# From the scan loops to the first expert: the order of projections, turnings and router products, and where softmax and selection stand

## The chip, the cores and the metric

The kernel runs on one core of a Trainium2 chip. The metric is the device time of one execution in microseconds (us), lower is better. Before the change three timed runs took 1291.97 us in the median (1289.67 to 1293.01). A further execution was profiled; all places in time below are us from the start of its span.

## The reference, cut to what matters

The block takes 512 tokens (8 batches of 64, width 512) through three parts, each added to the residual x: cross attention, a pair of Mamba tracks (fast and slow), and a mixture of eight experts, of which each token takes two.

```python
# end of the second part: two tracks, mixed, projected, added
combined = w[0] * fast_out + w[1] * slow_out
x = x + combined @ proj_w.T + proj_b
# third part, on xt = layernorm(x)
logits = xt @ Wr + br
p = softmax(logits); probs, idx = top_k(p, 2); probs = probs / probs.sum(-1)
h = layernorm(relu(xt @ W1[e] + b1[e])) * g1[e] + be1[e]
y = layernorm(relu(h @ W2[e] + b2[e])) * g2[e] + be2[e]
x = x + sum over the two experts of probs * y
```

## The kernel before, in words

All matrices are float32. 512 tokens are four chunks (NT) of 128; a width of 512 is four blocks (ND) of 128. TensorE (PE) multiplies, VectorE (DVE) and ScalarE (ACT) work on the results, GpSimd (POOL) and SyncE (SP) issue most DMAs.

**End of the Mamba part (L1126 to L1189).** The scan loops run over two tracks, eight channel blocks and six groups of states. After them come four output products (`rest_of`, m = 0 to 3) of the last channel block, each into one bank of two PSUM tiles of three banks: m = 0 and 1 into `das[0]`, m = 2 and 3 into `das[1]`. After each, DVE adds it to `comb[m]` (L1146). `projected(c)` then multiplies `comb` with `proj_w` for chunk c (L1159; `pp` alternates between the two single-bank tiles `mm` and `yp`), adds it to the residual `xr` on DVE (L1162) and normalizes it (L1164 to L1171, with the square root on ACT) into `l3`, which has the memory of `oT`. `routed(c)` turns the chunk with four PE transposes into the third bank of `das[c % 2]` (L1176), copies them on ACT to `xT` (L1177), multiplies with the router's matrix `wr` into a strip of the first bank of `das[0]` (L1180) and adds the bias on DVE to `pr` (L1183).

**The choice of experts (L1257 to L1403).** From `pr` of all chunks DVE finds the two best experts of a token (`hots`), counts (`upto`, with the PE products `rank` and `count`), and makes `take`, with which PE gathers the first expert's rows (`gp`, L1297, copied by ACT into `xgT0`, L1300). The rows of the others are scattered by eight indirect DMAs of POOL into `x_rows` in HBM (L1352) and fetched again expert by expert (`xg`, L1433). The softmax over the experts (`ex`, from L1371, exponential on ACT) is needed for the gates and for `share`.

**The experts.** Expert p has an `up` half (`hp` = L1470, activation on ACT L1477), twice; its centring, scaling and `down` (L1520) stand beside the next expert's `up`. Its rows are turned by PE at L1439. `selection()` makes, for the last expert, four `give` tiles on DVE (L1409), turns them on PE (L1413) and copies them on ACT into `put` (L1414); it is called in the second expert's first half.

**What sets the order.** Instructions wrapped in `keep(...)` stay on their engine in the order of the program among one another; the others are placed by the framework's scheduler, which weighs estimated times and dependences. Dependences are kept by tile: an instruction that writes one bank of `das[0]` waits for the reader of another bank of it. Tiles take turns in a fixed number of buffers. Weight loads of the experts are issued by SP (L1225, L1233); they use memory that the loops hold until the last router product.

Of the kernel before, what the change touches and what calls it, by code (L numbers as in the profile page):

```python
# [13 lines left out]
ALU = mybir.AluOpType  # L14
# [6 lines left out]
NT = T // P  # L21
ND = D // P
# [27 lines left out]
def perceiver_block(ctx: ExitStack, tc: tile.TileContext, a: dict, out: bass.AP):  # L50
    nc = tc.nc

    keep = tc.keep_in_program_order
# [7 lines left out]
    ident = const.tile([P, P], F32, name="ident")  # L61
# [152 lines left out]
    pr = const.tile([P, NT, E], F32, name="pr")  # L214
# [8 lines left out]
    def block(general):  # L223
# [4 lines left out]
        with ExitStack() as ctx:  # L228
# [594 lines left out]
            with tc.tile_pool(name="mb1", bufs=1) as mb1, tc.tile_pool(name="mb2", bufs=2) as mb2, tc.tile_pool(  # L823
# [304 lines left out]
                def rest_of(m, chunks):  # L1128
                    for i in chunks:
                        keep(nc.tensor.matmul(  # L1130
                            das[m // 2][:, m % 2, :], mos[m][:, i, :], xs[1][i], start=(i == m + 4), stop=(i == last)
                        ))
# [8 lines left out]
                    summed_up(q)  # L1141
                for m in range(2, ND):
                    rest_of(m, range(m + 4, last))
                for m in range(ND):
                    rest_of(m, [last])
                    keep(nc.vector.scalar_tensor_tensor(  # L1146
                        comb[m], das[m // 2][:, m % 2, :], tw[:, 1:2], comb[m], ALU.mult, ALU.add
                    ))
# [7 lines left out]
                def projected(c):  # L1156
                    pp = pm.tile([P, D], F32, tag=("mm", "yp")[c % 2], name="pp")
                    for k in range(ND):
                        keep(nc.tensor.matmul(  # L1159
                            pp, comb[k][:, c * P : (c + 1) * P], pws[k], start=(k == 0), stop=(k == ND - 1)  # L1160
                        ))
                    keep(nc.vector.tensor_tensor(xr[:, c, :], xr[:, c, :], pp, ALU.add))  # L1162
                    st = small.tile([P, 6], F32, tag="lnst1", name="lnst1")
                    keep(nc.vector.bn_stats(st, xr[:, c, :]))  # L1164
                    mv = small.tile([P, 2], F32, tag="lnmv1", name="lnmv1")
                    keep(nc.vector.bn_aggr(mv, st))
                    std = small.tile([P, 1], F32, tag="std1", name="std")
                    keep(nc.scalar.activation(std, mv[:, 1:2], AF.Sqrt, bias=eps))
                    rs = small.tile([P, 1], F32, tag="rs1", name="rs")
                    keep(nc.vector.reciprocal(rs, std))  # L1170
                    keep(nc.vector.tensor_scalar(l3[:, c, :], xr[:, c, :], mv[:, 0:1], rs, ALU.subtract, ALU.mult))  # L1171

                def routed(c):
                    tp = das[c % 2][:, 2, :]
                    for k in range(ND):
                        keep(nc.tensor.transpose(tp[:, k * P : (k + 1) * P], l3[:, c, k * P : (k + 1) * P], ident))  # L1176
                    keep(nc.scalar.copy(xT[:, c, :], tp))  # L1177
                    rp = das[0][:, 0, c * E : (c + 1) * E]
                    for k in range(ND):
                        keep(nc.tensor.matmul(  # L1180
                            rp, xT[:, c, k * P : (k + 1) * P], wr[:, k, :], start=(k == 0), stop=(k == ND - 1)
                        ))
                    keep(nc.vector.tensor_tensor(pr[:, c, :], br, rp, ALU.add))  # L1183

                projected(0)
                for c in range(1, NT):
                    projected(c)
                    routed(c - 1)
                routed(NT - 1)  # L1189

            mbx.close()

# [5 lines left out]
            with ExitStack() as moe:  # L1198
# [43 lines left out]
                with tc.tile_pool(name="mor", bufs=1) as mor:  # L1242
                    def over_e(t):
                        return t.rearrange("p (c o) -> p c o", o=1).to_broadcast([P, NT, E])
# [4 lines left out]
                    def tiny(name):  # L1249
                        return mor.tile([P, NT], F32, name=name)  # L1250

                    def wide(name, n=NT):
                        return mor.tile([P, n, E], F32, name=name)
# [3 lines left out]
                    hots, tops = [], []  # L1257
                    for i in range(2):
                        src = left if i else pr
                        m = tiny(f"top{i}")  # L1260
# [33 lines left out]
                    for k in range(ND):  # L1294
                        gp = pe.tile([P, CAP], F32, tag=("tp", "yp")[k % 2], name="gp")
# [72 lines left out]


                    ex = wide("ex")  # L1370
                    nc.vector.tensor_tensor(ex, pr, over_e(tops[0]), ALU.subtract)  # L1371
                    nc.scalar.activation(ex, ex, AF.Exp)
                    ls = tiny("ls")
                    nc.vector.tensor_reduce(ls, ex, AX.X, ALU.add)
# [30 lines left out]
                def selection():  # L1405

                    for c in range(NT):
                        give = mo2.tile([P, P], F32, tag="y", name="give")
                        nc.vector.tensor_scalar(  # L1409
                            give, iota[:, :P], place7[:, c : c + 1], share[:, c : c + 1], ALU.is_equal, ALU.mult  # L1410
                        )
                        gp = pe.tile([P, P], F32, tag="tp", name="gp7")
                        nc.tensor.transpose(gp, give, ident)  # L1413
                        nc.scalar.copy(put[:, c * P : (c + 1) * P], gp)  # L1414

                for p in range(1, E):
# [182 lines left out]
                def experts(todo):  # L1599
# [3 lines left out]
                    for p, s0 in todo + [(E, 0)]:  # L1603
# [8 lines left out]
                        for hf in range(2):  # L1612
                            if p < E:
                                up(hf, st)
                            if (p, s0, hf) == (1, 0, 0) and first:
                                selection()
                            if prev is not None and not (p == E and first and hf == 0):
                                for i in range(2):
                                    (center, scale)[hf](i, prev[2])
# [27 lines left out]
            with tc.If(rare > 0):  # L1647
# [10 lines left out]
                if not general:  # L1658
                    with tc.If(flag(found[0:1, 1:2], 1) > 0):
                        block(True)  # L1660

    block(False)


# [54 lines left out]
```

## Time and profile before

| | |
|---|---|
| timed runs, median (range) | 1291.97 us (1289.67 to 1293.01) |
| the profiled execution, its own time | 1286.84 us |
| its span in the trace | 1285.1 us |
| mean granted TensorE clock | 0.977 of full speed |
| PE busy | 1183.2 us (92%) |
| DVE busy | 800.9 us (62%) |
| ACT busy | 592.9 us (46%) |
| POOL busy | 502.2 us (39%) |

The profiled execution's own time is 1.74 us over its span and 5.13 us under the median of the timed runs. A float32 product appears in the trace as two passes (x2), and a wait in brackets behind an instruction is the idle time of its engine before it, with what ended it. PEld is PE's loading of weights, SPq the queue of SyncE.

### The profile page before, as it was taken

How to read it: one execution, taken by the hardware profiler on the slowest of the kernel's cores; microseconds unless marked ns; L12 is line 12 of the kernel's file. 1: busy time of each engine (PE TensorE's matmuls, PEld its weight loads, DVE VectorE, ACT ScalarE, POOL GpSimd, SP SyncE). 2: the span in 40 equal slices, each digit the busy share in tenths (PEclk: the TensorE clock that was granted, in tenths of full speed). 3: DMA queues.
4: the chain of work that ended last, by engine and by line, in shares of the span. 5: the costliest groups of instructions: out<-in, count | busy, mean ns of one | idle time of the engine just before them, and what ended most of it. 6: DMA issues, size and time to landing. Idle time of an engine off the chain costs nothing. (4 is left out here: it accounts for less than half of the span.)

```text
span 1285.1 us, 14205 instructions
## 1 busy us (share of the span) xinstructions
PE 1183.2 (92%) x5134; PEld 720.4 (56%) x5134; DVE 800.9 (62%) x1135; ACT 592.9 (46%) x1265; POOL 502.2 (39%) x353
## 2 busy tenths in 40 slices
PE   5999999999987899999899998978799999999996
PEld 5444454444543333334333333333589999999994
DVE  5144444444666999999999999995415244333363
ACT  2233334333227576677666665651126235334460
POOL 5100000000015688888798888870130201221102
PEclk9999999999988999999999999999799999999998
DMA  6429910000007110101431010010395725746634
GB/s 213 164 63 300 302 36 1 1 1 1 1 9 263 63 32 2 33 1 57 180 116 33 16 50 17 25 41 17 127 399 200 285 107 211 300 176 229 259 127 129
DMA packets 94160, 147.36 MB, mean 115 GB/s; under 512 B 5888, under 2 KB 63504, under 8 KB 89984
## 3 DMA queue, kind: packets, MB, share of 16 engines
q1 hardware_dynamic: 88496, 130.26, 29.6%
q0 software_dynamic: 4528, 14.00, 3.0%
q10 hardware_dynamic: 1056, 2.10, 0.5%
q8 instruction: 42, 0.69, 0.2%
q14 instruction: 38, 0.31, 0.1%
HBM read 121.80 MB, written 24.54 MB: 114 GB/s over the span
## 5 line engine op out<-in xcount | busy, mean ns | idle before, releaser
L1114 POOL TENSOR_TENSOR db<-r,bc 128x1536 f32<-128x1536 f32 (+1 forms) x96 | 294.8, 3077 | 51.1 <-DVE da L1076 34.8
L1076 DVE TENSOR_TENSOR_SCAN da<-da,db 128x1536 f32<-128x1536 f32 (+1 forms) x96 | 288.1, 3001 | 7.6 <-POOL db L1114 5.8
L1090 PE MATMUL yp<-hc,ident 128*128 128x512 f32 x512 | 239.8, 604 | 16.3 <-DVE hc L1080 16.3
L1110 ACT ACTIVATE da<-dt,an 128x504 f32<-128x504 f32 x256 | 175.3, 685 | 10.0 <-DVE dt L892 0.8
L1090 PEld LDWEIGHTS yp<-hc,ident 128*128 128x128 f32 x512 | 95.6, 191 | 149.3 <-issue 106.3
L1080 DVE TENSOR_TENSOR hc<-da,bc 128x1536 f32<-128x1536 f32 (+1 forms) x96 | 151.7, 1580 | 10.3 <-PE yp L1090 1.6
L1470 PE MATMUL hp<-xgT,w 128*128 128x192 f32 (+3 forms) x1024 | 147.6, 303 | 5.8 <-DVE xgT L1442 3.0
L1470 PEld LDWEIGHTS hp<-xgT,w 128*128 128x128 f32 x1024 | 143.0, 191 | 7.6 <-DVE xgT L1442 3.7
L1520 PE MATMUL yp<-h,w 128*128 128x192 f32 (+3 forms) x1024 | 146.4, 303 | 0.9 <-DMA w<-in_w_dram 0.6
L1520 PEld LDWEIGHTS yp<-h,w 128*128 128x128 f32 x1024 | 143.2, 191 | 2.3 <-ACT h L1500 0.8
L450 POOL COPY qbd<-qT 32x256 f32<-32x256 f32 x32 | 12.6, 395 | 214.0 <-PE sp L631 207.3
L1610 POOL DMA_DIRECT2D ev<-in_ev_dram x8 | 4.5, 569 | 231.8 <-ACT yT L1527 178.1
L460 PE MATMUL kp<-ctx,wk 128*128 128x400 f32 x256 | 93.6, 510 | 0.0
L617 PE MATMUL vp<-wv,ctx 128*128 128x512 f32 x192 | 88.2, 604 | 0.0
L1477 ACT ACTIVATE h<-hp,ev 128x192 f32<-128x192 f32 (+3 forms) x128 | 50.1, 393 | 77.5 <-PE hp L1470 77.0
L680 DVE COPY oT<-op 32x64 f32<-32x64 f32 x64 | 13.7, 214 | 96.7 <-PE op L669 96.3
L930 PE MATMUL ip<-oT,iw 128*128 128x512 f32 x128 | 61.2, 623 | 12.1 <-issue 5.4
L1105 ACT COPY da<-zeros 128x24 f32<-128x24 f32 (+1 forms) x96 | 16.9, 176 | 117.9 <-DVE hc L1080 117.9
L460 PEld LDWEIGHTS kp<-ctx,wk 128*128 128x128 f32 x256 | 46.3, 189 | 43.7 <-issue 13.7
L1537 DVE BATCH_NORM_STATS2 bs<-ytp 128x6 f32<-128x512 f32 (+3 forms) x13 | 8.5, 689 | 90.0 <-PE ytp L1535 90.0
L637 DVE CUSTOM_DVE_ANT_0 sc<-sp,madd,rsc 128x400 f32<-128x400 f32 x64 | 38.1, 629 | 40.4 <-PE sp L631 40.4
L1038 PE MATMUL cp<-x,mo 128*128 128x512 f32 x108 | 50.2, 598 | 7.9 <-ACT r L874 7.9
(292 smaller groups left out, 1617.7 us busy)
## 6 DMA issues: line engine op xcount, KB each, us to landing
w<-in_w_dram SPq DMA_DIRECT2D x64, 1024.0 KB, 15.8
bc<-bcd SPq DMA_DIRECT2D x8, 1536.0 KB, 9.4
x_rows<-z SPq DMA_DIRECT2D x8, 1152.0 KB, 12.1
y_rows<-z SPq DMA_DIRECT2D x8, 1152.0 KB, 12.2
ctx<-in_ctx_dram SPq DMA_DIRECT2D x32, 200.0 KB, 4.3
iw<-in_fast_in_w_dram SPq DMA_DIRECT2D x8, 512.0 KB, 6.6
iw<-in_slow_in_w_dram SPq DMA_DIRECT2D x8, 512.0 KB, 3.4
mo<-in_slow_mout_w_dram SPq DMA_DIRECT2D x8, 512.0 KB, 3.7
```

The source lines that it names most:

```text
L460: nc.tensor.matmul(kp[:, :n], wk[:, k, ec * P : (ec + 1) * P], ctx_t[k][:, o : o + n], start=(k == 0), stop=(k == ND - 1),)
L617: nc.tensor.matmul(vp, ctxs[b][k][:, j * P : (j + 1) * P], wv[:, k, :], start=(k == 0), stop=(k == ND - 1))
L930: keep(nc.tensor.matmul(s[key], w[:, k, u * P : (u + 1) * P], oT[k], start=(k == 0), stop=(k == ND - 1)))
L1038: keep(nc.tensor.matmul(s["cp"], mo[:, i, :], xs[t2][i], start=(i == 0), stop=(i == n - 1)))
L1076: keep(nc.vector.tensor_tensor_scan(hs, hs, q["db"][:, :w, :].rearrange("p n s -> p (n s)"), 0.0, ALU.mult, ALU.add))
L1080: keep(nc.vector.tensor_tensor(q["hc"][:, :w, :], q["da"][:, :w, :], bcs[t][1][n][:, 1], ALU.mult))
L1090: keep(nc.tensor.matmul(yp[0], ident, q["hc"][:, j, :], start=False, stop=(n + j == NS - 1)))
L1110: keep(nc.scalar.activation(by_batch(da[:, j, :])[:, :, 1:], by_batch(dt)[:, :, 1:], AF.Exp, scale=an[:, t, k : k + 1]))
L1114: keep(nc.gpsimd.tensor_tensor(db[:, :w, :], du.rearrange("p (o s) -> p o s", o=1).to_broadcast([P, w, T]), bc[:, 0], ALU.mult))
L1470: nc.tensor.matmul(hp, st["w1"][k][:, i * P : (i + 1) * P], st["xgT"][:, k, :n], start=(k == 0), stop=(k == ND - 1),)
L1477: nc.scalar.activation(h[:, i, :], hp, AF.Relu, bias=st["ev"][:, i : i + 1])
L1520: nc.tensor.matmul(yp, ws[i // 4][:, i % 4, m * P : (m + 1) * P], st["h"][:, i, :], start=(i == 0), stop=(i == NF - 1),)
```

## The change

Four edits in the stretch between the scan loops and the second expert:

- the four output products and combinations run in the order 0, 2, 1, 3, so that the two PSUM tiles take turns;
- `routed` is split: `turned(c)` holds the transposes and the copy to `xT`, `routed(c)` the router's product. Two projections come first, and then for each chunk its turning, the projection two chunks on, and its router product;
- the first instruction of the softmax (`ex`, L1371) is kept in program order, behind the other kept DVE work;
- the transposes of `selection` (L1413) are kept in program order too.

In the built kernel this moves, beyond the loops: on DVE the softmax and what hangs on it, from between the sums of `upto` to behind the last flag (`either`, L1367); on ACT the table load and exponential from before the copies of `xgT0` to between the third and fourth of them; on PE the four transposes of `selection` from among the first expert's first products to among the second expert's, near its mean; with them the copies to `put` on ACT and two of the four `give` on DVE. The queues of SP and POOL keep their order and their waits.

```diff
--- before.py
+++ after.py
@@ -1141,7 +1141,7 @@
                     summed_up(q)
                 for m in range(2, ND):
                     rest_of(m, range(m + 4, last))
-                for m in range(ND):
+                for m in (0, 2, 1, 3):
                     rest_of(m, [last])
                     keep(nc.vector.scalar_tensor_tensor(
                         comb[m], das[m // 2][:, m % 2, :], tw[:, 1:2], comb[m], ALU.mult, ALU.add
@@ -1170,11 +1170,13 @@
                     keep(nc.vector.reciprocal(rs, std))
                     keep(nc.vector.tensor_scalar(l3[:, c, :], xr[:, c, :], mv[:, 0:1], rs, ALU.subtract, ALU.mult))
 
-                def routed(c):
+                def turned(c):
                     tp = das[c % 2][:, 2, :]
                     for k in range(ND):
                         keep(nc.tensor.transpose(tp[:, k * P : (k + 1) * P], l3[:, c, k * P : (k + 1) * P], ident))
                     keep(nc.scalar.copy(xT[:, c, :], tp))
+
+                def routed(c):
                     rp = das[0][:, 0, c * E : (c + 1) * E]
                     for k in range(ND):
                         keep(nc.tensor.matmul(
@@ -1182,11 +1184,14 @@
                         ))
                     keep(nc.vector.tensor_tensor(pr[:, c, :], br, rp, ALU.add))
 
+
                 projected(0)
-                for c in range(1, NT):
-                    projected(c)
-                    routed(c - 1)
-                routed(NT - 1)
+                projected(1)
+                for c in range(NT):
+                    turned(c)
+                    if c + 2 < NT:
+                        projected(c + 2)
+                    routed(c)
 
             mbx.close()
 
@@ -1368,7 +1373,7 @@
 
 
                     ex = wide("ex")
-                    nc.vector.tensor_tensor(ex, pr, over_e(tops[0]), ALU.subtract)
+                    keep(nc.vector.tensor_tensor(ex, pr, over_e(tops[0]), ALU.subtract))
                     nc.scalar.activation(ex, ex, AF.Exp)
                     ls = tiny("ls")
                     nc.vector.tensor_reduce(ls, ex, AX.X, ALU.add)
@@ -1410,7 +1415,7 @@
                             give, iota[:, :P], place7[:, c : c + 1], share[:, c : c + 1], ALU.is_equal, ALU.mult
                         )
                         gp = pe.tile([P, P], F32, tag="tp", name="gp7")
-                        nc.tensor.transpose(gp, give, ident)
+                        keep(nc.tensor.transpose(gp, give, ident))
                         nc.scalar.copy(put[:, c * P : (c + 1) * P], gp)
 
                 for p in range(1, E):
```

## The prediction

> **What bounds the kernel now.** I read the page first (PE is busy 92% of the span), then the chain of waits in order of time. From 939.85 us to the end that chain is PE's, nearly without a break; in the stretch that the change touches, 884 to 940 us, it hops between PE, DVE and ACT. So I read this stretch instruction by instruction. From the timeline (start, duration, engine, line, operation, tiles, then idle time before it and who ended it):
>
> ```profile
> 885.97 1.98 PE L1130 MATMUL da<-x,mo 128*128 128x512 f32 x4 [0.84 <-DVE comb L1146]
> 887.13 1.61 DVE L1146 SCALAR_TENSOR_TENSOR comb<-da,tw,comb 128x512 f32<-128x512 f32 x2 [1.22 <-PE da L1130]
> 888.80 1.12 PE L1130 MATMUL da<-x,mo 128*128 128x512 f32 x2 [0.84 <-DVE comb L1146]
> ...
> 896.62 0.60 PE L1176 MATMUL da<-ident,oT 128*128 128x128 f32 x4
> 898.70 0.57 ACT L1177 COPY xT<-da 128x512 f32<-128x512 f32 x1
> 899.31 1.06 PE L1180 MATMUL da<-wr,xT 128*128 128x8 f32 x8 [2.09 <-ACT xT L1177]
> 900.23 5.38 PE L1159 MATMUL pp<-pw,comb 128*128 128x512 f32 x8
> 908.19 1.06 PE L1180 MATMUL da<-wr,xT 128*128 128x8 f32 x8 [2.15 <-ACT xT L1177]
> 909.10 3.68 PE L1159 MATMUL pp<-pw,comb 128*128 128x512 f32 x8
> 915.37 1.06 PE L1180 MATMUL da<-wr,xT 128*128 128x8 f32 x8 [2.15 <-ACT xT L1177]
> 917.59 1.87 PE L1180 MATMUL da<-wr,xT 128*128 128x8 f32 x8 [0.68 <-ACT xT L1177]
> ```
>
> PE stands twice for a combination (L1146) before it may write the neighbouring bank of the same tile, and three times some 2.1 us for xT, since the router's product is queued right behind the turning that feeds it. Nothing else runs: DVE and ACT are on the same thread.
>
> Then the start of the first expert, and the gather of the second expert's rows with its landing (last line: the list of DMA issues; last number is us to landing):
>
> ```profile
> 934.66 0.38 PE L1413 MATMUL gp<-ident,give 128*128 128x128 f32 x2
> 937.63 0.27 ACT L1414 COPY put<-gp 128x128 f32<-128x128 f32 x1 [1.21 <-PE hp L1470]
> 939.00 0.27 ACT L1414 COPY put<-gp 128x128 f32<-128x128 f32 x1 [1.10 <-PE hp L1470]
> 939.37 0.73 ACT L1477 ACTIVATE h<-hp,ev 128x192 f32<-128x192 f32 x2
> 939.85 10.34 PE L1470 MATMUL hp<-xgT,w 128*128 128x192 f32 x62 [2.25 <-ACT h L1477]
> 951.23 1.12 POOL L1433 DMA_DIRECT2D xg<-x_rows  x2 [12.96 <-DMA w<-in_w_dram]
> 958.89 1.86 PE L1439 MATMUL xtp<-ident,xg 128*128 128x128 f32 x8
> ...
> xg<-x_rows POOLq DMA_DIRECT2D x3, 256.0 KB, 6.1
> ```
>
> The selection's transposes and copies stand among the first expert's products; its activation waits behind them on ACT, and the third product waits for that. And the second expert's rows are close behind PE: issued at 951.23 and 951.78, landed by 957.9 if these too take 6.1 us, used at 958.89.
>
> **The change, part by part** (us in the frame of this execution).
>
> 1. Combinations 0, 2, 1, 3. A product is two passes of 0.43. Products 0 and 2 now run from 884.00 without a wait (different tiles). Combination 0 ends at 885.91 as before; product 1 starts at 885.97. Product 2, from 884.86, is out 1.16 later as product 0 was (884.00 to 885.16), so combination 2 ends 886.77 and product 3 starts at 886.85 instead of 888.80. The first projection follows at 887.85 instead of 889.76: **-1.9**. If the second wait stayed: -0.8.
>
> 2. Loops. Before: projection 0, 1, turn 0, router 0, projection 2, and so on. After: p0 p1 t0 p2 r0 t1 p3 r1 t2 r2 t3 r3. Start of t0: 16 passes after p0, at 894.73 (l3 of chunk 0 is out at 894.24, the row's 896.14 less 1.9: no wait). t0 0.57, p2 3.44 (eight passes of 0.43), r0 at 898.74: xT of chunk 0 is out at 899.27 less 1.9 = 897.4, so no wait. r0 0.8, t1 0.57, p3 3.44 end at 903.55; xT of chunk 1 stands behind std of chunk 2 on ACT (about 900.9), done by 901.5: no wait. r1 ends 904.4. Here comes a new wait. t2 writes the tile that r1 has just written, and pr of chunk 1 must read it first; on DVE's queue that reading now stands behind the whole normalization of chunk 3, which takes 3.0 from the end of p3 (rows: 912.82 to 915.63, plus pr 0.16). So t2 starts about 906.7, PE idle 2.3; queued behind it are r2, t3 and r3, and for r3 waits the whole expert stage. Then t2 to r2 1.3, r2 0.85, t3 to r3 1.3 (row: 916.28 to 917.59): r3 at 910.15 instead of 917.59. Of these 7.4, 1.9 are part 1's: **-5.5**. In it are two waits of 2.1 that vanish, 1.9 that p2 loses at present (5.38 against 3.44, at half clock, below), and a longer end (r1's end to r3 5.75, where p3's end to r3 took 4.97). Bounds: -3.0 if p2 had been at full clock anyway and r2 falls into a half-clock stretch (0.85 more); -6.4 if r3 runs at full clock.
>
> What waits for r3: the first weight load of the experts on SP (919.59, idle until then on the router's product) and ev on POOL's queue. Neither queue changes its order. So loads, scatter and gather move with r3.
>
> 3. Softmax held back. Its subtraction, and with it 12 small DVE operations, leave the chain to "take". The fourth sum (L1279) goes from 923.45 to about 923.03, and the division of the gates (L1387) no longer stands between: gp some 0.2 earlier, **-0.2**, between 0 and -0.5. On ACT the exponential's table load (1.28) and the exponential (0.23) now stand between the third and fourth copy of xgT0. Hidden: the fourth is needed only by the fourth product step, some 2 us after gp's end; without that cover it costs at most 0.6.
>
> 4. Selection held back. From 933.2 to 939.85 PE passes 16 products at 0.163 and four transposes: 3.1 us of work in 6.6. Without transposes and copies the products take 2.6, so up to 3.3 is won at the first expert. But PE would come to L1439 at 958.89 less all this, and the rows move only with parts 1 to 3. Their slack is 1.0 (957.9 against 958.89): **-0.9**, the rest becomes a wait for the rows of about 2.4. Bounds 0 and -3.3.
>
> 5. Selection's new place: in the order of the built kernel PE's queue now holds two transposes after the second expert's mean product (975.67) and two after half of the next tile. The first two cost 0.22. The third waits for its "give" on DVE, which stands behind the sum of squares (976.67, 0.96) and runs to about 978.0: PE, there at 977.75, waits 0.3; the fourth 0.3 more; then the second variance product waits for a DVE sum moved back by two "give" (0.7). By adding: products that stood at 979.03 stand at 979.98: **+0.95**. Queued behind: the sigma, scale and down-projection follow 0.8 later, still ahead of PE. Bounds: 0.45 (the four transposes' work alone) and 3.3 (what they cost at the old place).
>
> Sum: -1.9 - 5.5 - 0.2 - 0.9 + 0.95 = **-7.55**. The profiled execution took 1286.84 (span 1285.1 and 1.74 outside it); it becomes 1279.3. The median 1291.97 lies 5.13 above that execution, and I keep the distance: 1284.4. After 960 us PE is busy 97 to 99% and the loads are released by its progress, so the gain is carried to the end.
>
> **Clock.** From the windows view (PE busy, ..., then granted clock, DMA share, GB/s):
>
> ```profile
> 897.00:900.40 3.40, 1.31 (x12) 1.09 (x10) 2.10 (x5) 0.77 (x2) 0.00 (x0) 1.00 0.00 0
> 900.40:903.80 3.40, 3.40 (x5) 1.39 (x5) 0.16 (x1) 0.00 (x0) 0.00 (x0) 0.52 0.00 0
> 914.10:917.50 3.40, 1.55 (x12) 1.31 (x12) 1.20 (x5) 1.31 (x3) 0.00 (x0) 1.00 0.00 0
> 917.50:920.90 3.40, 1.87 (x8) 1.78 (x8) 1.23 (x8) 0.65 (x2) 0.78 (x2) 0.51 0.30 39
> ```
>
> Here stretches with PE busy 1.31 and 1.55 of 3.4 were followed by half clock, and no wait in them was longer than 2.4. [...]
>
> **Rivals.** (a) The wait for the rows halves the clock: a wait of 2.4 can leave a stretch like those two; the next 3.4 at half clock costs 1.7: 1286.1. For: the rows above. Against: only if part 4 really wins its 3.3, and by the place of the stretch.
> (b) Rows come earlier than PE needs (the scatter is faster, or the wait at t2 is shorter): part 4 gives up to 3.3: about 1282.
> (c) Loops gain less (-3.0) and the selection costs 3.3 at its new place: -1.9 - 3.0 - 0.2 - 0.9 + 3.3 = -2.7: 1289.3. For: transposes in PE's queue with DVE and ACT between them are what cost 3.3 at present.
> (d) Slower: the rows do not move. From 935 to 960 the DMA engines are full (shares 1.00 to 1.06), and the gather stood 12.96 on POOL. If the scatter's landing is set by the bytes already queued and not by its issue, PE wins only 0.9, stands over 7 us at L1439, then runs at half clock (13.65 us of it, as from 917.5 to 931.2, costs up to 6.8), and pays 0.95: +0.05 to +6.8: 1292 to 1299, about 1296. It decides once the rows land less than 3 us earlier. Against: the bytes ahead of the scatter are released by r3 as well.
> (e) The loops give nothing: what is taken from xT comes back in full at the turnings behind pr. Then 5.5 of the 7.55 is gone: 1289.9.
>
> **Numbers.** Forecast 0.46, (a) 0.22, (b) 0.08, (c) 0.12, (d) 0.08, (e) 0.04. A measurement of this kernel can tell 0.3% (3.9 us) from no change, so faster is below 1288.1 and slower above 1295.9. Faster: forecast, (a), (b) and a little of (c): 0.78. Same: most of (c), (e), a third of (d): 0.17. Slower: 0.05. Range 1280.5 to 1290.5: down to (b) less the 1.5 of a clock kept full at r3, up to (c) and (e); (d) is left out.
>
> **What would show it.** PE's waits for xT at the first two router products gone; a wait of some 2.3 at the third turning, ended by DVE pr; SP's first weight load about 7.4 earlier, at 912.2; no "put" among the first expert's products and its first activation about 3 us sooner after gp; a wait at L1439 (L1444 then) for the rows, which land about 7.6 earlier; transposes of the selection near the second expert's mean with waits under 1 us in all. Wrong if the first weight load is less than 5 us earlier, if t2 starts without a wait, if the rows land less than 5 us earlier, or if PE loses over 2 us at the selection's new place.

## The result and the profile after

Five executions of each kernel: before 1290.2 us median (1289.3 to 1293.01), after 1283.92 us (1281.8 to 1287.98); after/before 0.9947, 95% interval [0.9923, 0.997]. Timed again, with the second pair of profiles below: 1287.29 before, 1279.44 after, 0.994 [0.9919, 0.996].

The first profile of the changed kernel is of the slowest of its five executions (1287.98 us), and it was already 1.9 us behind the profile of before at the scan's last products, where nothing is changed; so the two are compared by distances inside a stretch. First the timeline of PE in it (start, duration, engine, line, operation, tiles, idle time before it and who ended that):

```profile
884.92 4.97 PE L1130 MATMUL da<-x,mo 128*128 128x512 f32 x10
889.73 7.03 PE L1159 MATMUL pp<-pw,comb 128*128 128x512 f32 x16
...
900.47 0.95 PE L1182 MATMUL da<-wr,xT 128*128 128x8 f32 x8
...
905.18 0.95 PE L1182 MATMUL da<-wr,xT 128*128 128x8 f32 x8
908.32 0.65 PE L1176 MATMUL da<-ident,oT 128*128 128x128 f32 x4 [2.18 <-DVE pr L1185]
909.64 1.88 PE L1182 MATMUL da<-wr,xT 128*128 128x8 f32 x8 [0.68 <-ACT xT L1177]
911.37 1.09 PE L1176 MATMUL da<-ident,oT 128*128 128x128 f32 x4
913.14 1.88 PE L1182 MATMUL da<-wr,xT 128*128 128x8 f32 x8 [0.67 <-ACT xT L1177]
...
927.02 2.11 PE L1475 MATMUL hp<-xgT,w 128*128 128x192 f32 x12
930.59 0.89 PE L1475 MATMUL hp<-xgT,w 128*128 128x192 f32 x4 [1.46 <-DMA w<-in_w_dram]
935.00 1.33 PE L1475 MATMUL hp<-xgT,w 128*128 128x192 f32 x3 [3.52 <-ACT h L1482]
```

The combinations' two waits are gone (ten passes, which are five products, in one row), and so are the first two waits for xT. The third turning has the new wait, 2.18 for DVE pr. From 909.55 on the windows view gives a granted clock of 0.50: 1.88 for a router product that takes 0.95 in the row at 905.18. At the end stands something that the prediction has not: PE is through with the first 16 passes of the first expert at 931.5 by its own records, and the first activation is not until 934.52 (the last row is cut by the end of the window asked for). The timeline of ACT in the same profile shows it, and the same once more at the very end of the kernel:

```profile
934.52 0.73 ACT L1482 ACTIVATE h<-hp,ev 128x192 f32<-128x192 f32 x2 [6.53 <-remote]
...
1268.74 0.37 ACT L1532 ACTIVATE yT<-yp,ev 128x128 f32<-128x128 f32 x1 [7.66 <-remote]
```

"Remote" is a releaser that the profile can't name. PE's last records before these two end at 931.5 and 1264.6, 3.0 and 4.2 earlier. The first profile of before has the same at these two places, 1.8 at each. So both kernels were profiled once more; there neither profile has these delays. This second pair (1287.41 us before, 1278.82 after, spans 1285.75 and 1277.16) is the clean one. In it the first weight load of the experts (SPq), the first activation (ACT), and PE at the first and second expert, the kernel before:

```profile
920.39 10.42 SPq L1225 DMA_DIRECT2D w<-in_w_dram  x8
937.24 0.73 ACT L1477 ACTIVATE h<-hp,ev 128x192 f32<-128x192 f32 x2
...
934.13 1.46 PE L1470 MATMUL hp<-xgT,w 128*128 128x192 f32 x8
935.43 0.38 PE L1413 MATMUL gp<-ident,give 128*128 128x128 f32 x2
935.65 0.82 PE L1470 MATMUL hp<-xgT,w 128*128 128x192 f32 x4
936.31 0.51 PE L1413 MATMUL gp<-ident,give 128*128 128x128 f32 x2
936.66 0.82 PE L1470 MATMUL hp<-xgT,w 128*128 128x192 f32 x4
937.71 10.34 PE L1470 MATMUL hp<-xgT,w 128*128 128x192 f32 x62 [0.24 <-ACT h L1477]
...
958.25 0.33 PE L1439 MATMUL xtp<-ident,xg 128*128 128x128 f32 x1 [1.34 <-DMA xg<-x_rows]
959.18 2.41 PE L1439 MATMUL xtp<-ident,xg 64*128 64x64 f32 x7 [0.60 <-DMA xg<-x_rows]
961.52 4.21 PE L1470 MATMUL hp<-xgT,w 128*128 128x192 f32 x12
```

and the changed kernel:

```profile
914.56 10.24 SPq L1230 DMA_DIRECT2D w<-in_w_dram  x8
931.25 0.73 ACT L1482 ACTIVATE h<-hp,ev 128x192 f32<-128x192 f32 x2 [2.30 <-PE hp L1475]
...
927.99 2.96 PE L1475 MATMUL hp<-xgT,w 128*128 128x192 f32 x16
931.73 10.34 PE L1475 MATMUL hp<-xgT,w 128*128 128x192 f32 x62 [0.78 <-ACT h L1482]
...
951.99 0.34 PE L1444 MATMUL xtp<-ident,xg 128*128 128x128 f32 x1 [1.00 <-DMA xg<-x_rows]
952.95 1.66 PE L1444 MATMUL xtp<-ident,xg 64*128 64x64 f32 x7 [0.62 <-DMA xg<-x_rows]
954.53 2.22 PE L1475 MATMUL hp<-xgT,w 128*128 128x192 f32 x12
...
970.26 0.38 PE L1418 MATMUL gp<-ident,give 128*128 128x128 f32 x2
970.48 0.82 PE L1462 MATMUL var<-s,mean_f 128*128 128x192 f32 x4
971.13 0.81 PE L1475 MATMUL hp<-xgT,w 128*128 128x192 f32 x4
971.90 0.55 PE L1418 MATMUL gp<-ident,give 128*128 128x128 f32 x2
```

Read them against the prediction: at the old place the selection's four transposes stand among the first expert's products, and the first activation comes 16.85 after the first weight load; without them, in the changed kernel, 16.69. So they cost next to nothing (3.3 was predicted to hang on them). At their new place no row has a wait for give. PE waited for the second expert's rows in the kernel before too (1.34 and 0.60), and after it the products ran at half clock (4.21 against 2.22 for the same twelve passes). The windows view (PE busy first; granted clock, DMA share and GB/s last), the stretch with that wait and the next one, before and after:

```profile
955.88:959.30 3.42, 1.48 (x9) 1.00 (x7) 0.00 (x0) 0.62 (x2) 0.10 (x1) 1.00 1.07 349
959.30:962.71 3.41, 3.41 (x11) 2.29 (x12) 2.43 (x4) 0.00 (x0) 0.81 (x2) 0.50 1.02 340
```

```profile
949.65:953.07 3.42, 1.80 (x11) 1.32 (x9) 0.00 (x0) 0.84 (x2) 0.09 (x1) 1.00 1.05 342
953.07:956.48 3.41, 3.41 (x19) 2.78 (x20) 2.36 (x4) 0.00 (x0) 1.08 (x2) 1.00 1.04 351
```

The ledger of the second pair, each row a difference of two starts in PE's timeline (the last rows by ACT's):

| distance | before | after | change | predicted |
|---|---|---|---|---|
| first product of the slow scan's output projection (da, L1130) to first projection (pp) | 12.78 | 10.82 | -1.96 | -1.9 |
| first projection to last router product | 27.83 | 23.42 | -4.41 | -5.5 |
| last router product to first product of the first expert's gather (gp) | 7.41 | 7.17 | -0.24 | -0.2 |
| that to the second expert's first transpose (xtp) | 32.45 | 32.26 | -0.19 | -0.9 |
| that to the first expert's second mean product | 7.27 | 4.60 | -2.67 | 0 |
| that to the second expert's first mean product | 13.25 | 12.95 | -0.30 | 0 |
| that to the first expert's first yT (selection's new place in it) | 17.12 | 17.72 | +0.60 | +0.95 |
| first yT to end | 289.86 | 289.90 | +0.04 | 0 |
| upstream of all this | | | +0.55 | |
| sum | | | -8.58 | -7.55 |

### The profile page after: what moved, and what is told of

Read it like the earlier page. It is cut to its first block, busy times and chain, and to the rows that moved or that the text cites. A ratio compares the mean times of both kernels' runs of the same rounds, so it can differ in the third digit from the quotient of the medians.

```text
span 1286.2 us, 14209 instructions
## 1 busy us (share of the span) xinstructions
PE 1183.3 (92%) x5134; PEld 722.6 (56%) x5134; DVE 802.3 (62%) x1135; ACT 592.2 (46%) x1265; POOL 502.2 (39%) x353
## 5 line engine op out<-in xcount | busy, mean ns | idle before, releaser
L1475 PE MATMUL hp<-xgT,w 128*128 128x192 f32 (+3 forms) x1024 | 150.2, 306 | 8.5 <-ACT h L1482 4.0
L1475 PEld LDWEIGHTS hp<-xgT,w 128*128 128x128 f32 x1024 | 145.6, 193 | 10.6 <-ACT h L1482 4.6
```

Source lines behind the costliest of these rows:

```text
L1475: nc.tensor.matmul(hp, st["w1"][k][:, i * P : (i + 1) * P], st["xgT"][:, k, :n], start=(k == 0), stop=(k == ND - 1),)
```

## The experiments

Times are in us; each ratio is against the kernel before on the same chip (e1 to e6 and the second pair on one chip, e7 to e9 on a second, e10 on a third; one profile of each). "da to r3" is the distance in PE's timeline from the first product of the slow scan's output projection to the last router product, "load" the first weight load of the experts.

**e1, the orders alone; e2, the held-back operations alone.**

```diff
 e1 (changed kernel)                        e2 (kernel before)
-keep(nc.vector.tensor_tensor(ex, ...))    +keep(nc.vector.tensor_tensor(ex, ...))
+nc.vector.tensor_tensor(ex, ...)          -nc.vector.tensor_tensor(ex, ...)
-keep(nc.tensor.transpose(gp, give, ...))  +keep(nc.tensor.transpose(gp, give, ...))
+nc.tensor.transpose(gp, give, ...)        -nc.tensor.transpose(gp, give, ...)
```

> The kernel before with parts 1 and 2 alone (order of the combinations, and the order of the loops); softmax and selection are as before. Theory A (the prediction's steps): third turning waits about 2.2 for DVE pr, first weight load of the experts 6.4 earlier against the last scan product than before, selection's transposes still among the first expert's products, and the first activation 19.8 after the first weight load as before; after the first expert about 0.8 of the gain is kept more than in the changed kernel, because nothing is paid at the second expert: about -7.4 against before in all. Theory B (the first expert starts when its own four weight tiles are in, 15.4 after the first load, and the selection's place is not what sets it): the same distances, about -6.4 + 0.9 less the half clock: 1284 to 1285.5. The two part in e2, not here; what this run must show by both is a gain within 1.5 us of the changed kernel's, and if it is under 3 us the loops are not the source of the gain.

> The kernel before with softmax and selection held back alone (parts 3, 4, 5). Theory A: without transposes and copies among the first expert's products its first activation comes about 16.5 after the first weight load (19.8 before), and PE then waits about 2.3 at the second expert's transposes for its rows, whose landing does not move. Total -0.2, plus up to 1.7 if that wait halves the clock. Theory B: first activation still 19.4 after the first weight load, no wait for the rows, the cost of the selection at its new place remains: +0.5 to +0.9, and up to 2.6 more if the wait for the weights falls so that the clock is halved after it.

e1: 1280.17, 0.9938 [0.9923, 0.9953]. e2: 1288.09, 1.0004 [0.9995, 1.0013]. The gain is the orders' alone. From the load to the first activation it is 16.62 in e1 (transposes among the products) and 16.33 in e2 (transposes gone): theory A's 19.8 for e1 fell; its 16.5 for e2 came out, but e1 has it with the transposes in place, so it is no gain of moving them; theory B's size (19.4) fell too. In e2 PE waits there for the fourth weight tile. Its timeline:

```profile
931.86 2.11 PE L1470 MATMUL hp<-xgT,w 128*128 128x192 f32 x12
935.64 0.89 PE L1470 MATMUL hp<-xgT,w 128*128 128x192 f32 x4 [1.67 <-DMA w<-in_w_dram]
936.72 10.34 PE L1470 MATMUL hp<-xgT,w 128*128 128x192 f32 x62 [0.19 <-ACT h L1477]
...
957.20 0.33 PE L1439 MATMUL xtp<-ident,xg 128*128 128x128 f32 x1 [1.21 <-DMA xg<-x_rows]
```

The tile is in 15.7 after the load (919.92), the first activation follows at 936.25, and then PE waits for the rows, which have not moved. Half clock followed that wait in e1 as in e2 (granted clock 0.50 from 952.29 to 955.70 in e1, from 958.83 to 962.24 in e2).

**e3, the router's product in the tile of its own turning.**

```diff
-rp = das[0][:, 0, c * E : (c + 1) * E]
+rp = das[c % 2][:, 0, c * E : (c + 1) * E]
```

> The changed kernel with the router's product of chunk c written to the tile das[c % 2] in place of das[0], so that the third turning no longer shares its tile with the second chunk's router product. If the wait of 2.2 at the third turning is for pr of chunk 1 because both stand in one tile, it goes, PE's wait at the fourth turning is then under 0.5, and the first weight load comes 1.5 to 2.5 earlier against the last scan product; everything behind moves with it: 1.5 to 2.5 faster than the changed kernel. Rival: the wait comes back at the router's product of chunk 2 (xT's copy behind std on ACT) or at the fourth turning: under 0.5 in all.

1277.69, 0.9925 [0.9912, 0.9938]. PE's timeline:

```profile
902.43 0.95 PE L1182 MATMUL da<-wr,xT 128*128 128x8 f32 x8
903.24 0.63 PE L1176 MATMUL da<-ident,oT 128*128 128x128 f32 x4
905.18 1.06 PE L1182 MATMUL da<-wr,xT 128*128 128x8 f32 x8 [1.31 <-ACT xT L1177]
906.09 0.74 PE L1176 MATMUL da<-ident,oT 128*128 128x128 f32 x4
907.50 1.87 PE L1182 MATMUL da<-wr,xT 128*128 128x8 f32 x8 [0.68 <-ACT xT L1177]
```

The third turning no longer waits: its wait came from the shared tile. Part of it returns as the 1.31 for xT (0.68 in the changed kernel); "da to r3" goes from 34.23 (second profile of the changed kernel) to 31.35, 2.9 where 1.5 to 2.5 was expected, because the router product of chunk 2 now falls before the half clock (1.06 for 1.88). The median is 1.75 under that of the changed kernel below, timed on another occasion, and the intervals overlap.

**e4, the first expert's weights in halves of their columns.**

```diff
-first_w1 = load_w1(0)
+first_w1 = [mo1.tile([P, F], F32, tag="w1", bufs=8, ...) for k in range(ND)]
+for f in range(0, F, F // 2):
+    for k in range(ND):
+        nc.sync.dma_start(first_w1[k][:, f : f + F // 2], a["w1"][0, k * P : ..., f : f + F // 2])
```

> The changed kernel with the first expert's four weight tiles loaded in halves of their columns, all four first halves before the second ones; same bytes. Theory B (landing of the weights sets the start): the first halves are in about 8 after the first load, before PE comes to the first product (11.9 after it), so the first activation comes about 13 after the first weight load instead of 19.4 and PE runs on without the half clock of 933 to 940; then the second expert's rows, which do not move, are late by about 4: 2 to 4.5 faster than the changed kernel in all. Theory A (the weights are not what it waits for): first activation still 19 or more after the first load and no change over 0.5.

1278.03, 0.9921 [0.9906, 0.9936]. The wait for the tile is gone, but the first activation comes 15.6 after the load, not 13: the gather's products, in part at half clock (7.3 for 32 passes; e9 below has 5.47 at full clock), hold the first product until 12.3, and its 16 passes follow. Two limits stand here a microsecond apart, so lifting one wins about one. It is not shown to be faster than the changed kernel: the intervals overlap.

**Both kernels profiled again.**

> The changed kernel once more, because its first profile was of its slowest execution and held two stalls (3.0 at the first expert's first tile, 4.2 at the last expert's last tile) in which PE's results reached ACT that much after PE's last record; the runs e1 to e4 show neither. Theory B': those stalls belong to the execution and not to the change; then the first activation comes 16.3 to 16.6 after the first weight load (about 1 after the fourth weight tile is in), PE waits 1.2 and 0.6 for the second expert's rows, which land 37.4 after the first weight load, and time is 1279.5 to 1281.5 on the chip of e1, 0.5 to 0.9 above e1. Theory A' (the change makes them): both stalls are there again, and the first activation comes over 19 after the first load.

> The kernel before once more, for its profile on the same chip. Theory B': the first activation also comes 16.3 to 16.6 after the first weight load although the selection's transposes stand among the products (19.8 in the first profile), and PE waits about 1.8 for the second expert's rows, where the first profile had no wait. Theory A: 19.5 to 20 again, and no wait for the rows.

Changed: 1279.44, 0.994 [0.9919, 0.996], load to first activation 16.69, waits for the rows 1.00 and 0.62. Before: 16.85, and 1.34 and 0.60. Theory B' holds in both in kind, a little above the 16.3 to 16.6 that it gave, with a shorter wait in before than the 1.8 expected; A and A' fall. The median of the changed kernel was expected 0.5 to 0.9 above that of e1 and is 0.73 below it, within the intervals. The half clock behind the wait for the rows is in the profile of before (0.50 from 959.30 to 962.71) and not in that of the changed kernel (1.00 from 953.07 to 956.48).

**e5, the first expert's down-projection weights behind the second expert's rows** (on e3).

```diff
-nc.sync.dma_start(w, of_turn(a["w2"][...], p)...)
+src = of_turn(a["w2"][...], p)...
+if p: nc.sync.dma_start(w, src)
+else: keep(nc.gpsimd.dma_start(w, src))
...
+rows_in = nc.gpsimd.dma_start(xg[:m, u, :], x_rows[r0 : r0 + m, :])
+if p == 1 and s0 == 0: keep(rows_in)
```

> e3 with the first expert's four tiles of the down-projection's weights (4 MB, used only some 65 after the first weight load) issued by POOL behind the gather of the second expert's rows, instead of by SP ahead of the scatter's landing. If the bytes ahead of them set when the rows land (DMA moves 380 to 430 GB/s in that stretch), the rows land 3 to 8 earlier against the first weight load (37.8 in e3), PE's waits of 1.57 and 0.70 for them go, and the kernel is 2.0 to 2.5 faster than e3, more where e3 falls into the half clock there. Rival: the scatter's own issue on POOL (eight of 1.26) sets the landing: the rows land less than 1 earlier and nothing over 0.5 is won.

1273.06, 0.9884 [0.9862, 0.9905]: the best version here. In PE's timeline the transposes follow without a wait:

```profile
938.91 8.29 PE L1479 MATMUL hp<-xgT,w 128*128 128x192 f32 x50
947.03 1.86 PE L1448 MATMUL xtp<-ident,xg 128*128 128x128 f32 x8
```

From the load to the first of them 35.99 where e3 had 37.81. The gather is issued only 0.4 earlier (31.5 after the load; 32.0 in e3), but it lands 3.3 after its issue where it took 5.8 in e3 beside those 4 MB: the rows are there 3.0 earlier, at the low end of the 3 to 8 expected, and 1.2 before PE uses them. So the rival had the scatter right, and the expected gain came from another part of the way. From the load to the first expert's first yT it is 70.51 against 73.14: 2.6 of the 4.6 between the medians is seen here; e3 was timed on another occasion, so the rest is not assigned.

**e6 and e7, e5 with the selection, then with selection and softmax, not held back.**

```diff
 e6, e7
-keep(nc.tensor.transpose(gp, give, ident))
+nc.tensor.transpose(gp, give, ident)
 e7 only
-keep(nc.vector.tensor_tensor(ex, pr, over_e(tops[0]), ALU.subtract))
+nc.vector.tensor_tensor(ex, pr, over_e(tops[0]), ALU.subtract)
```

> e5 with the selection not held back (part 5 undone): its transposes stand among the first expert's products again, where PE waits for the fourth weight tile anyhow. If the old place costs nothing there and the new one costs 0.6 (e2 and e3 against e1 and before, from the second expert's mean product to the first expert's yT: 17.72 against 17.12), this is 0.6 faster than e5. Rival: at the old place the transposes delay the first activation by up to 3.3, as the first profile had it: up to 2.7 slower than e5.

> e5 with neither softmax nor selection held back, so that parts 3 and 5 are both undone. In e6 the selection was back at its old place but its give stood behind the held-back softmax on DVE, and PE waited 1.78 for it ahead of the first expert's last weight tile. If that is the whole reason, the first activation comes 16.4 to 16.9 after the first weight load again (18.3 in e6), the selection costs nothing at the first expert and the 0.6 at the second expert is saved; the softmax costs 0.2: 0.2 to 0.6 faster than e5. Rival: the transposes cost at the old place by themselves: the first activation over 17.5 after the first load and 1 or more slower than e5.

e6: 1277.31, 0.992 [0.9902, 0.9938]. Its profile has a wait that neither old nor new place had:

```profile
929.49 0.65 PE L1420 MATMUL gp<-ident,give 128*128 128x128 f32 x2 [1.78 <-DVE give L1416]
```

"give" stands behind the held-back softmax on DVE, so the two edits of the change belong together: 18.29 from the load to the first activation. By distances from the first product of the slow scan's output projection, e6 is 0.6 later than e5 at the first yT and 0.8 more behind it; 2.7 was there upstream, in unchanged work. e7: 1280.92, 0.9935 [0.9922, 0.9947], on another chip, and with the late results in its profile (first activation 19.51 after the load, PE's records ending 2.6 before it). Its profile can't be compared with that of e5, and its ratio is above that of e5 (0.9884): no gain is shown, and whether the last 0.6 is to be had stays open.

**e8 and e10, the two orders apart.**

```diff
 e8 (kernel before)                e10 (changed kernel)
-for m in range(ND):              -for m in (0, 2, 1, 3):
+for m in (0, 2, 1, 3):           +for m in range(ND):
     rest_of(m, [last])                rest_of(m, [last])
```

> The kernel before with part 1 alone, the order of the last combinations. The first projection follows 1.9 to 2.0 earlier against the scan's last products, and r3, the first weight load and everything behind it move by the same: -1.9, about 0.15%. Rival: the second wait for a combination stays, -0.8; or the router's chain gives it back because a half-clock stretch falls elsewhere: between -3.5 and +1.5 in all, seen in the clock's row.

> The changed kernel with the combinations in their old order (part 1 undone); loops, softmax and selection as changed. Part 1 alone (e8) brought the first projection 1.96 earlier and the last router product only 0.33, the rest went into a longer half clock. If the new loops keep the 1.96, this kernel's first projection is 1.9 to 2.0 later than in the changed kernel and the last router product is later by the same: against the scan's last products 36.1 to 36.3 to the last router product (34.24 changed, 40.62 before), and 1.5 to 2.5 slower than the changed kernel in all. If the loops alone give the 6.4 and the order of the combinations nothing, the last router product is within 0.5 of the changed kernel's.

e8: 1289.01, 0.9993 [0.9977, 1.0009], no gain that can be seen, though the interval also holds the 1.9 expected. e10: 1281.09, 0.9954 [0.9936, 0.9972]; against the changed kernel the intervals overlap. What the times can't part, the profiles do, one of each: with the second pair they make a square, "da to r3":

| | old loops | new loops |
|---|---|---|
| combinations 0, 1, 2, 3 | 40.62 | 36.65 |
| combinations 0, 2, 1, 3 | 40.29 | 34.23 |

The order of the combinations brings the first projection 1.96 earlier in both columns, but in these profiles it is worth 0.33 with the old loops and 2.42 with the new ones (the 36.65 of e10 is 0.4 over what was expected: its third turning runs at half clock already, 1.11 for 0.66). PE's timeline of e8 shows where the rest goes:

```profile
895.74 0.60 PE L1176 MATMUL da<-ident,oT 128*128 128x128 f32 x4
898.42 1.88 PE L1180 MATMUL da<-wr,xT 128*128 128x8 f32 x8 [2.09 <-ACT xT L1177]
900.15 6.20 PE L1159 MATMUL pp<-pw,comb 128*128 128x512 f32 x8
```

The half clock that followed the first wait for xT lasted 6.8 (898.42 to 905.24) in place of 3.4 (900.51 to 903.92 in the first profile of before) and took the router product (1.88 for 1.06) and the next projection (6.20 for 5.38) with it. The new loops have no wait there (e10). This is one profile, and two of one kernel can differ in where the half clock falls: the first expert's 62 passes took 12.92 in the first profile of the changed kernel and 10.34 in the second.

**e9, PE kept busy** (on e5): products nobody reads behind the third and fourth turning and four behind the last router product.

```diff
+def filled(pool, n, times):
+    fill = pool.tile([P, D], F32, tag="mm", name="fill")
+    for _ in range(times):
+        keep(nc.tensor.matmul(fill[:, :n], ident, l3[:, 0, :n], start=True, stop=True))
...
+else: filled(pm, D if c + 1 < NT else D // 2, 1)
...
+filled(pe, D, 4)
```

> e5 with products that nobody reads (ident by l3) put where PE waits: one of 128x512 behind the third turning, one of 128x256 behind the fourth, four of 128x512 behind the last router product. If a stretch of 3.4 with little PE work is what halves the clock, the 13.7 of half clock from about the third turning to the gather's products are gone: the router's products of chunk 2 and 3 and the turnings run at full clock and the first weight load comes 0.8 to 1.7 earlier against the scan; the products of the gather take 5.2 to 5.4 where they took 8.1; but the first activation still comes 16 to 16.5 after the first weight load, because the fourth weight tile sets it: 0.8 to 1.7 faster than e5, and no 2.8 from the gather's products. Rival: the first expert is set by the gather's products: 3.5 or more faster; or the fill is in the way of the turning and the choice: no gain, the first load not earlier.

1280.3, 0.9935 [0.9919, 0.9952], on the chip of e7, with the late result at the end (3.5). The clock stayed full from the turnings to the gather's products (1.00 in the windows view from 906.50 to 923.50; e5 has 0.71, 0.50 and 0.50 from 906.50 to 916.70). Of PE's timeline:

```profile
915.02 5.47 PE L1312 MATMUL gp<-take,oT 128*128 128x192 f32 x32 [0.73 <-DVE take L1308]
...
922.01 0.89 PE L1487 MATMUL hp<-xgT,w 128*128 128x192 f32 x4 [0.22 <-DMA w<-in_w_dram]
925.46 14.11 PE L1487 MATMUL hp<-xgT,w 128*128 128x192 f32 x66 [2.56 <-DMA w<-in_w_dram]
```

The load is 0.95 earlier, the gather's products take 5.47 (8.07 in e5), and the first activation still comes 16.63 after the load: what the gather wins, PE waits for the fourth tile, 2.56, and after that wait the products run in part at half clock (14.11 for 66 passes, where 62 take 10.34 in e5; granted clock 0.69 from 923.50 to 926.90). At the first yT it is 1.5 later than e5, counted from the scan's output projection: no gain.

## Why the prediction was right, step by step

The gain is there because its largest part, the orders, was right. The five terms add up to -7.55, and their rows in the ledger to -6.20. That the median (1283.92) came out within 0.5 of the forecast (1284.4) is partly luck: 7.55 was taken off a median of 1291.97, which two more executions brought to 1290.2, and the difference of the medians is 6.28. In the second pair it is 7.85 between the medians and 8.58 between the profiles, and of the latter -2.97 is the clock behind the wait for the rows, which the sum put at nothing.

- **Combinations, -1.9: shown** (-1.96). That it adds to the loops was taken for granted; in the one profile of e8, alone it is worth 0.33 at the last router product.
- **Loops, -5.5: mechanism right, term mis-sized** (-4.41). Both waits for xT vanish and the wait at the third turning is there (2.18 and 2.17 for 2.3). What was off is the clock: the sum put only the last router product at half clock; in both profiles the half clock began before the router product of chunk 2, so that one (1.88) and the fourth turning (1.09) took about double too. That is one of the two conditions of the bound -3.0; the other, the projection of chunk 2 at full clock before the change, was not met. e3 confirms the cause of the new wait.
- **Softmax, -0.2: shown** (-0.24).
- **Start of the first expert, -0.9 capped from 3.3: wrong step.** The 3.3 was read off a row in which the copies to put stand 1.4 apart, as the transposes' price. In the second profile of before the same copies go without such gaps and the first activation comes 16.85 after the load; the orders alone (e1) have 16.62 with the transposes there, the changed kernel 16.69 without them. And the first profile of the changed kernel has 19.37 without them. So the 3.3 was the late results of that profile, not the transposes' price. Where the gather's products end early (e2, e9, e10, the first profile of the changed kernel), PE waits for the fourth weight tile (15.4 to 15.7 after the load); in the second pair they end late, in part at half clock, and leave next to no wait for the tile. The two limits lie about a microsecond apart (e4). The sign that the prediction named for this step, the first activation about 3 sooner after gp, did not come: 11.44 and 11.52 in the second pair. The cap was right, and even too generous: PE can use the rows only 37 to 38 after the load in the second pair and in e1 to e3, and it waited for them before the change as well; the term was -0.19.
- **Selection's new place, +0.95: right in kind**, +0.60. The waits for give that the sum counted are not in the rows; the size is near its lower bound, the transposes' own work (0.45). With that, softmax and selection held back give nothing together (e2: 1.0004).
- **Clock after the wait for the rows.** Rival (a) has it as a loss of the change; the sum puts it at nothing, and no run shows that such a wait costs no clock. The wait is there on both sides; in the second pair half clock followed it in the kernel before (4.21 for twelve passes; -2.67 and -0.30 in the ledger) and not in the changed one (2.22). The first pair has no wait for the rows at all, since with the late results PE came to them later (39.3 and 41.5 after the load); in it the changed kernel's half clock fell at the first expert's start (933.4 to 940.3), and before had none there. No run shows that the change decides it: e1, with the orders alone, has the half clock behind this wait too, and e3, with a wait of 1.57, has not.
- **Carried to the end: shown** (+0.04 from the first yT on). PE's busy share behind 960 was read too high, though: in the windows it is 94 to 100% up to 1260 and 50% in the last 25.
- **The signs of error that the prediction named.** The first weight load came 6.4 earlier in the first pair (distance from the scan's output projection), over the 5 named; t2 waits; the rows' landing moved with the load (in the second pair PE uses them 6.8 earlier), so rival (d) fell; the selection's new place costs 0.60, under the 2 named.

## What to carry to other kernels

A gap that a profile lays beside an instruction is not that instruction's price: ask what else ended there (here results that reached ACT late, and a weight tile that lands at the same time), and profile again when a releaser is one that it can't name. Two edits on one path need not be a sum: the orders took 0.33 and 3.97 off "da to r3" alone and 6.39 together, with the half clock in different places; four kernels, none, one, the other and both, say more than two differences. And when everything hangs on one early load, moving that load moves the whole; work in its shadow can be free at the old place too (16.85 from load to first activation with the transposes, 16.69 without).

## What the runs showed of the hardware

**Late results.** In five of the fourteen profiles (both first ones, e7, e8, e9) the last tile of the last expert reaches ACT 1.8 to 4.2 after PE's last record, and in four of them (not e9) the first expert's first activation begins 1.8 to 3.0 after; in the nine others, the same two kernels among them, neither is over 0.4. e7 to e9 ran on one chip and the nine on two others, so the chip may be the reason, though that of the first pair is not known; how the delay comes about was not found out.

**The clock.** In the windows view of the first pair the granted clock is 0.50 from 900.51 to 903.92 (3.41) and from 917.58 to 931.23 (13.65) in the kernel before, from 909.55 to 923.20 (13.65) and from 933.44 to 940.27 (6.83) in the changed one. What PE did just before such a change is seen at the wait for the rows, in stretches of 3.41 or 3.42 at full clock. With PE busy 1.48, 1.57 and 1.59 of them (second profile of before, e1, e2) the next one is at 0.50; with 1.80 (second profile of after) and 1.84 (e3) it is at 1.00. Busy time alone does not settle it: stretches with 2.00 and 2.77 (e10, e4), filled largely by 64x64 transposes, were followed by 0.50 as well, and one of the same kind with 2.72 in e3 was not (the mean product behind it took 0.81, where it took 1.05 in e1). Two rows of the windows view of e8 say the same:

```profile
898.42:901.83 3.41, 3.41 (x10) 2.54 (x11) 0.42 (x2) 0.00 (x0) 0.00 (x0) 0.50 0.00 0
905.24:908.65 3.41, 1.55 (x7) 0.69 (x5) 1.73 (x5) 0.53 (x2) 0.00 (x0) 1.00 0.00 0
```

In the first PE is busy throughout, 1.88 of it with the 128x8 router product, and half clock goes on behind it (6.20 for the projection in e8's rows above, where the next takes 3.68). The second, with the end of a projection in it, was followed by full clock at busy 1.55 (1.06 for the router product at 908.94), where the prediction's row at 914.10, also 1.55 but with a router product, was followed by 0.51. Why the clock changed in the one case and not in the other, no run here takes apart.
